# Conditional low-rank residual on one core: the second outer product of the first pair of blocks split into seven, and its sums divided between Pool and DVE

## The chip, the core and the metric

The kernel runs on one core of one Trainium2 chip. The metric is the device time of one execution in microseconds (us). The kernel before was timed three times; the comparison is with the median of those runs. A separate profiled execution gives the page and the trace that every duration below comes from.

## The reference

The input is 64 sequences of 64 tokens with 1024 features, 4096 tokens in all, in float32. Two layers follow each other, and each adds its result to its input:

```python
# layer 0: per sequence one adapter out of 64, rank 16
Bx = einsum('bni,bri->bnr', x, B[adapter_ids])
x = x + einsum('bnr,bor->bno', Bx, A[adapter_ids])
# layer 1: a dense product and eight gated experts of rank 16
base = einsum('btd,od->bto', x, W)
logits = einsum('btd,ed->bte', x, Wr) + 5.0 * one_hot(language_ids)
gates = softmax of the two largest logits, 0 elsewhere
h = einsum('btd,erd->bter', x, A1)
x = x + base + 2.0 * einsum('bter,bte,eor->bto', h, gates, B1)
```

The dense product with the 1024 x 1024 matrix W is most of the arithmetic.

## The kernel before

**Layout.** The kernel holds x with features on the partitions and tokens along the free axis. The 4096 tokens are eight blocks of 512, and two blocks make a pair; the variable s counts the four pairs, k the eight blocks. W lies in SBUF as sixteen tiles `w_ij` of 128 x 2 x 256. The identity is added to the four diagonal ones (`add_identity`), so that the dense product already contains the residual.

**Work per block.** `gather` (line 367) fetches the adapter's rows with an indirect DMA that Pool issues (`gb` for B, `ga` for A). `turn` transposes `gb` on TensorE (tiles `pt`), ScalarE (ACT) copies that to `bt`; `project` (line 400) multiplies it with x (tile `pb` out of `bt`, 64 small matmuls) and DVE masks the result to `bx`; `adapt` (line 428) multiplies `bx` with `ga` (tiles `px`) and DVE adds it to x in place. These steps are `early`. Then `rows` (line 466) multiplies x with the expert matrices and the gate matrix side by side (tiles `ph`), ACT copies the result to `h`, `gates` (line 504) is a chain of some twenty small DVE instructions that finds the two largest logits and scales `h`, and `weigh` (line 564) transposes `h` (tile `pg`) into `hg`. These are `late`.

**The dense product, twice by seven.** Of a pair, the product of a 2 x 2 arrangement of weights (halves of the outputs and of the features) with a 2 x 2 arrangement of tokens (halves of the features and the two blocks) is made with seven products and sums in place of eight. These are the outer products n, made in the order `ORDER` = 1, 2, 6, 7, 5, 3, 4. Their weights `m_q[n]` are sums of the quarters of W (`outer`, line 639); their tokens are x itself or sums of x: T3 = x_b[1] - x_b[0], T2 = T3 + x_a[0], T4 = x_a[1] - T2 and, in place, x_b[0] - x_a[0] (`token_sum`, line 696, four DVE instructions of 128 x 512 each; in the profile `t<-x,x`, `t<-t,x`, `t<-x,t`, `x<-x,x`). Each outer product is made in the same way again out of seven inner products k (`product`, line 833): each is eight matmul records of 128 x 256 in the trace, the two halves of the features for two groups of outputs, two records to each matmul instruction. The inner sums are

- of weights: `weights` (line 660), four instructions for each n, tiles `s_n5`, `s_n6`, `s_n7`, `s_n3` (profile: `s<-w,w`, `s<-s,w`, `s<-w,s`). They depend on W alone, so they are made in the first pair only, stored to DRAM (`s_kept`, DMAs that SP issues) and loaded again by the later pairs;
- of tokens: `inner_tokens` (line 718), four instructions for each n, tiles `ti_n5`, `ti_n6`, `ti_n7`, `ti_n4` (profile: `ti<-t`, `ti<-t,ti`, `ti<-x`, `ti<-x,ti`), made in every pair.

After a product, `leave` (line 866) adds what stands in PSUM to an output or to the sums `u` and `v`, on DVE, or on ACT where it is a plain copy. A PSUM tile `pa` gathers k = 1, 6, 5 and 3 and is read between these, so that each next one of them waits for the reading. Where an outer product takes part in one of the four results, four of its inner products carry two more matmuls with `b1_sb`, which add the experts (`hg`, or differences `hd`, `he` of it from `gate_sum` and `gate_diff`).

**Whole products.** An outer product that is named in `WHOLE` (line 250) is not split: `whole_product` (line 804) makes it in four parts with 128 x 512 matmuls (tiles `pw`), eight records each and two more with `b1_sb`. `WHOLE` has pair 0 with n = 1 and with n = 2. Their inner weight sums are made nevertheless, since the later pairs load them.

**What sets the order.** Nothing is issued by hand. Every step goes to a planner (class `Plan`, line 34) with the engines that may take it and its assumed cost there, the tiles that it reads and writes, the buffers that it takes and a due time `at`. `order` (line 64) goes through an assumed time and gives each engine the ready step that can start first, the earlier due time deciding between those that can start within 0.2; a step with two engines goes to the one where it can start first. The assumed cost of two SBUF-to-SBUF steps on DVE and Pool at once is raised. The result is one fixed order for each engine's queue. Buffers have fixed numbers (`slots`, line 256): two for each of `t5`, `t6`, `t7`, `t4` (the tiles `ti`), seven for `q` (halves of a block of x, and the sums T), two for PSUM `a`, two for `b`, two for `gb` and `ga`. A step that takes a buffer waits for the last reader of what was in it. `SLOTS` = 49 is the distance of two pairs in due times.

In the first pair the sums have the engines `BOTH` (DVE 0.7 or Pool 1.3); in the later pairs the inner token sums are Pool's. The driver at lines 988 to 1025 sets the due times; line 1009 is T4.

Of the kernel before, what the change touches and what calls it, by code (L numbers as in the profile page):

```python
# [177 lines left out]
def kernel(  # L178
# [68 lines left out]
    ORDER = (1, 2, 6, 7, 5, 3, 4)  # L247
    SLOTS = 49

    WHOLE = {(0, 1), (0, 2)}  # L250

    pe, dve = Pinned(tc, nc.tensor), Pinned(tc, nc.vector)
    act, pool, sp = Pinned(tc, nc.scalar), Pinned(tc, nc.gpsimd), Pinned(tc, nc.sync)
# [14 lines left out]
    def new(tag, shape, name):  # L268
        return pools[tag].tile(shape, F32, tag=tag, name=name)
# [74 lines left out]
    def part(t, cs=range(HC), gs=range(NG)):  # L344
        return [(t, c, g) for c in cs for g in gs]
# [7 lines left out]
    def load(k, i, at):  # L353
        t = ("x", k, i)

        def fn(e):
            made[t] = new("q", [P, HC, TB], f"x_{k}_{i}")
            sp.dma_start(
                made[t],
                xT[i * HC * P : (i + 1) * HC * P, k * TB : (k + 1) * TB].rearrange(  # L360
                    "(c p) t -> p c t", p=P
                ),
            )

        plan.add({"SP": 0.5}, fn, [], part(t), at, [("q", t)], kb=1024)

    def gather(k, tag, table, at):
        def fn(e):
            made[tag, k] = new(tag, [P, D], f"{tag}_{k}")
            pool.indirect_dma_start(  # L370
                out=made[tag, k],
                out_offset=None,
                in_=table,
                in_offset=bass.IndirectOffsetOnAxis(ap=idx[:, k : k + 1], axis=0),
            )

        plan.add({"POOL": 1.1}, fn, [], [((tag, k),)], at, [(tag, (tag, k))], kb=512)
# [204 lines left out]
    def early(k, at):  # L582
        turn(k, 0, at)
        turn(k, 1, at)
        project(k, at + 2)
        adapt(k, 0, at + 3)
        adapt(k, 1, at + 4)

    def late(k, at):
        rows(k, at)  # L590
        gates(k, at)
        weigh(k, at + 6)
# [32 lines left out]
    def combine(out, a, b, op, at, engines):  # L625

        fresh = out not in (a, b)

        def fn(e):
            if fresh:  # L630
                made[out] = new("s", [P, QC, QO], "_".join(str(p) for p in out))
            engine[e].tensor_tensor(made[out], made[a], made[b], op)

        plan.add(engines, fn, [(a,), (b,)], [(out,)], at, [("s", out)] * fresh, sb=True)

    DVE = {"DVE": 0.7}
    BOTH = {"DVE": 0.7, "POOL": 1.3}

    def outer(n, at):

        if n == 5:
            m_q[5] = {k: ("m5",) + k for k in quarter[1, 0]}
            for k in m_q[5]:
                combine(m_q[5][k], quarter[1, 0][k], quarter[1, 1][k], ALU.add, at, DVE)
        elif n == 7:
            m_q[7] = quarter[1, 0]
            for k in m_q[7]:
                combine(m_q[7][k], quarter[0, 0][k], m_q[7][k], ALU.subtract, at, DVE)
        elif n == 6:
            m_q[6] = quarter[0, 0]  # L650
            for k in m_q[6]:
                combine(m_q[6][k], m_q[5][k], m_q[6][k], ALU.subtract, at, DVE)
        elif n == 3:
            m_q[3] = quarter[0, 1]
            for k in m_q[3]:
                combine(m_q[3][k], m_q[3][k], m_q[6][k], ALU.subtract, at, DVE)
# [3 lines left out]
    def weights(s, n, at):  # L660

        out = {}
        if s > 0:
            for i, m in enumerate(ORDER):
                out[m] = t = ("s", s, n, m)

                def fn(e, t=t, m=m):
                    made[t] = new("s", [P, QC, QO], f"s_{s}_{n}{m}")
                    sp.dma_start(made[t].rearrange("p c o -> p (c o)"), s_kept[n - 1, m - 1])

                plan.add({"SP": 0.1}, fn, [("kept", n, m)], [(t,)], at + i - 8, [("s", t)], kb=256)
            wt[n] = out
            return
        m = m_q[n]
        out = {1: m[0, 0], 2: m[0, 1], 4: m[1, 1]}
        for k, (u, v, op) in {
            5: ((1, 0), (1, 1), ALU.add),
            6: (5, (0, 0), ALU.subtract),
            7: ((0, 0), (1, 0), ALU.subtract),
            3: ((0, 1), 6, ALU.subtract),  # L680
        }.items():
            out[k] = ("s", s, n, k)
            uu = m[u] if isinstance(u, tuple) else out[u]
            vv = m[v] if isinstance(v, tuple) else out[v]
            combine(out[k], uu, vv, op, at - 4, BOTH)
        for k in ORDER:
            t = out[k]

            def keep(e, t=t, k=k):
                sp.dma_start(s_kept[n - 1, k - 1], made[t].rearrange("p c o -> p (c o)"))  # L690

            plan.add({"SP": 0.1}, keep, [(t,)], [("kept", n, k)], at + 4, kb=256)
        wt[n] = out


    def token_sum(s, n, at):

        xa, xb = [("x", 2 * s, i) for i in range(2)], [("x", 2 * s + 1, i) for i in range(2)]
        u, v, op = {
            3: (xb[1], xb[0], ALU.subtract),  # L700
            2: (("t", s, 3), xa[0], ALU.add),
            4: (xa[1], ("t", s, 2), ALU.subtract),
            1: (xb[0], xa[0], ALU.subtract),
        }[n]
        t = xb[0] if n == 1 else ("t", s, n)
        for c in range(HC):

            def fn(e, c=c):
                if c == 0 and n != 1:
                    made[t] = new("q", [P, HC, TB], f"t_{s}_{n}")  # L710
                dve.tensor_tensor(made[t][:, c], made[u][:, c], made[v][:, c], op)

            plan.add(
                DVE, fn, part(u, [c]) + part(v, [c]) + (part(t, [0]) if c else []), part(t, [c]),
                at, [("q", t)] * (c == 0 and n != 1), sb=True,
            )

    def inner_tokens(s, n, m, at):
        def b(i, j):
            return made[m][:, i * QC : (i + 1) * QC, j * HT : (j + 1) * HT]  # L720

        def keys(i, j):
            return part(m, range(i * QC, (i + 1) * QC), range(2 * j, 2 * j + 2))

        out = {k: (("view", i, j), keys(i, j)) for k, i, j in ((1, 0, 0), (2, 1, 0), (3, 1, 1))}
        for k, u, v in ((5, (0, 1), (0, 0)), (6, (1, 1), 5), (7, (1, 1), (0, 1)), (4, (1, 0), 6)):
            t = ("ti", s, n, k)

            def fn(e, t=t, k=k, u=u, v=v):
                made[t] = new(f"t{k}", [P, QC, HT], f"ti_{s}_{n}{k}")  # L730
                vv = b(*v) if isinstance(v, tuple) else made["ti", s, n, v]
                engine[e].tensor_tensor(made[t], b(*u), vv, ALU.subtract)

            vk = keys(*v) if isinstance(v, tuple) else [(("ti", s, n, v),)]
            plan.add(
                {"POOL": 1.3} if s else BOTH, fn, keys(*u) + vk, [(t,)], at - 5,
                [(f"t{k}", t)], sb=True,
            )
            out[k] = (t, [(t,)])
        ti[n] = {  # L740
            k: ((lambda t=t: b(*t[1:])) if t[0] == "view" else (lambda t=t: made[t]), ks)
            for k, (t, ks) in out.items()
        }
# [33 lines left out]
    def products(s):  # L777
# [10 lines left out]
        def at():  # L788
            return s * SLOTS + slot[0]
# [131 lines left out]
        def begin(n):  # L921
            dest.setdefault(n, n)
            if s == 0 and n in (6, 3):
                outer(n, at() - 4)
            weights(s, n, at() + (6 if (s, n) in WHOLE else 0))
            if s == 0 and n == 2:
                outer(5, at() + 4)
                outer(7, at() + 8)
            if (s, n) in WHOLE:
                whole_h[n] = {2: ("hg", ka), 3: ("hg", kb), 7: ("hg", kb), 4: ("he", s)}.get(n)  # L930
# [31 lines left out]
        for n in ORDER:  # L962
            after = ORDER[ORDER.index(n) + 1] if n != ORDER[-1] else None
            if (s, n) in WHOLE:
                for k in rest:
# [35 lines left out]
    for s in range(NSUP):  # L1001
        k0 = 2 * s
        a0_ = s * SLOTS
        if s == 0:
            late(0, -14)
        late(k0 + 1, a0_ + 4 * (s > 0))
        token_sum(s, 3, a0_ + 3)
        token_sum(s, 2, a0_ + 5)
        token_sum(s, 4, a0_ + (18 if s == 0 else 7))
        token_sum(s, 1, a0_ + 20)  # L1010
        products(s)
        if s + 1 < NSUP:
            k0, k1 = k0 + 2, k0 + 3
            gather(k0, "gb", b0, a0_ + 8)
            gather(k0, "ga", a0, a0_ + 9)
            load(k0, 0, a0_ + 9)
            load(k0, 1, a0_ + 14)
            early(k0, a0_ + 17)
            late(k0, a0_ + 23)
            gather(k1, "gb", b0, a0_ + 22)  # L1020
            gather(k1, "ga", a0, a0_ + 23)
            load(k1, 0, a0_ + 22)
            load(k1, 1, a0_ + 29)
            early(k1, a0_ + 32)
# [48 lines left out]
```

## Time and profile before

| | |
|---|---|
| time, three runs | 528.14, 528.67, 529.69 us; median 528.67 |
| profiled execution, its own time | 528.18 us |
| its span | 526.4 us (1.78 us lie around it) |
| TensorE clock granted | 0.998 |
| PE (matmuls) busy | 507.3 us, 96% of the span |
| PEld (weight loads) busy | 433.9 us, 82% |
| DVE busy | 290.1 us, 55%, 554 instructions |
| Pool busy | 182.8 us, 35%, 149 instructions |
| ACT busy | 41.1 us, 8% |
| DMA | 99.19 MB, 188 GB/s in the mean |

How to read it: times are counted from the start of the span. A group is named by line, engine, operation and tiles, out before in; all compute instructions have line 29, the recording helper, so a group is known by its tiles. Since matmuls are pipelined, the duration of a matmul group reaches beyond the start of the next; what a product costs is read from start to start. In the view of waits a row says which engine waited for what, the sum in us, how often, and the longest.

### The profile page before, as it was taken

To read this page: it belongs to the slowest core of one execution; us is meant where nothing else is said; L and a number is where in the kernel's file an instruction comes from. 1 tells how busy PE (TensorE), PEld (TensorE's weight loads), DVE (VectorE), ACT (ScalarE), POOL (GpSimd) and SP (SyncE) were. 2 spreads that over 40 slices of the span, in tenths; PEclk is the share of its full clock that TensorE was granted. 3 is DMA by queue.
4 is the path that set the end of the run, shared out by engine and by line. 5 is a ranking of instruction groups with operands and counts; after the bars stand their busy time and mean duration, and the time that the engine had idled before them with its cause. 6 is when DMAs were issued, how large, how long until landed. Compare 5 with 4: busy or idle time off the path is not lost.

```text
span 526.4 us, 8463 instructions
## 1 busy us (share of the span) xinstructions
PE 507.3 (96%) x3400; PEld 433.9 (82%) x3400; DVE 290.1 (55%) x554; ACT 41.1 (8%) x81; POOL 182.8 (35%) x149
## 2 busy tenths in 40 slices
PE   2899999999999999999999999999999999999995
PEld 1755768798888988898888998889888898888884
DVE  0639999948964174616674355345567417432632
ACT  1111010002000100011000100000200010001000
POOL 3231955762343234222333313312422323433200
PEclk9999999999999999999999999999999999999999
DMA  8999735768666249735566526743546633610222
GB/s 291 362 364 401 273 135 189 271 226 305 217 202 210 82 113 321 262 106 184 177 190 207 184 82 212 268 159 122 164 161 197 207 92 103 216 42 1 80 81 80
DMA packets 53687, 99.19 MB, mean 188 GB/s; under 512 B 4880, under 2 KB 10000, under 8 KB 53648
## 3 DMA queue, kind: packets, MB, share of 16 engines
q1 hardware_dynamic: 51344, 90.26, 51.6%
q0 software_dynamic: 2304, 8.39, 4.4%
q8 instruction: 27, 0.44, 0.4%
q14 instruction: 12, 0.10, 0.0%
HBM read 69.01 MB, written 29.62 MB: 187 GB/s over the span
## 4 chain that ended last, share of the span: by engine, by line
PE 95%; DMA 2%; DVE 1%; issue 1%; SPq 0%; ACT 0%
PE pa L29 37%; PE pb L29 36%; PE ph L29 11%; PE pw L29 6%; PE px L29 3%; DMA ids_sb<-in_ids 2%; PE pt L29 1%; PE pg L29 1%; SPq L29 0%; DVE o L29 0%; DVE bias L29 0%; ACT o L29 0%; DVE lang L29 0%; DVE bx L29 0%
## 5 line engine op out<-in xcount | busy, mean ns | idle before, releaser
L29 PE MATMUL pa<-ti,s 128*128 128x256 f32 x416 | 99.0, 381 | 0.7 <-ACT o L29 0.7
L29 PE MATMUL pb<-ti,s 128*128 128x256 f32 x376 | 93.4, 380 | 0.0
L29 PEld LDWEIGHTS pa<-ti,s 128*128 128x128 f32 x416 | 77.6, 190 | 12.1 <-ACT o L29 1.1
L29 PEld LDWEIGHTS pb<-ti,s 128*128 128x128 f32 x376 | 70.7, 190 | 9.5
L29 POOL TENSOR_TENSOR ti<-x,ti 128x512 f32<-128x512 f32 x28 | 37.1, 1326 | 85.3 <-PE pb L29 84.3
L29 PEld LDWEIGHTS ph<-a_sb,x 128*128 128x128 f32 x512 | 62.7, 190 | 3.8 <-issue 2.7
L29 PE MATMUL ph<-a_sb,x 128*128 128x136 f32 x512 | 63.3, 279 | 2.1 <-issue 2.1
L29 POOL TENSOR_TENSOR ti<-t,ti 128x512 f32<-128x512 f32 x24 | 33.5, 1396 | 87.3 <-PE pb L29 64.9
L29 POOL TENSOR_TENSOR ti<-x 128x512 f32<-128x512 f32 x26 | 34.1, 1310 | 53.0 <-PE pb L29 31.6
L29 DVE TENSOR_TENSOR o<-pb,o 128x512 f32<-128x512 f32 x45 | 31.0, 690 | 34.1 <-PE pb L29 20.6
L29 PE MATMUL pa<-x,s 128*128 128x256 f32 x208 | 49.8, 379 | 0.0
L29 DVE TENSOR_TENSOR x<-px,x 128x512 f32<-128x512 f32 x64 | 39.8, 682 | 10.4 <-PE px L29 6.1
L29 POOL TENSOR_TENSOR ti<-t 128x512 f32<-128x512 f32 x22 | 29.4, 1339 | 44.1 <-PE pb L29 34.5
L29 PEld LDWEIGHTS pa<-x,s 128*128 128x128 f32 x208 | 38.7, 190 | 4.8
L29 PE MATMUL pa<-t,s 128*128 128x256 f32 x168 | 41.3, 382 | 0.8 <-DVE o L29 0.8
L29 PEld LDWEIGHTS pa<-t,s 128*128 128x128 f32 x168 | 31.4, 190 | 5.7 <-DVE o L29 1.2
L29 DVE TENSOR_TENSOR o<-pa,u 128x512 f32<-128x512 f32 x28 | 19.3, 691 | 26.8 <-PE pa L29 26.3
L29 PE MATMUL pw<-x,w 128*128 128x512 f32 x64 | 28.7, 595 | 0.0
L29 DVE TENSOR_TENSOR u<-pb,u 128x512 f32<-128x512 f32 x21 | 14.5, 689 | 25.5 <-ACT u L29 20.7
L29 PE MATMUL pb<-hg,b_sb 128*128 128x256 f32 x88 | 26.2, 379 | 0.0
L29 DVE TENSOR_TENSOR o<-pa,v 128x512 f32<-128x512 f32 x16 | 11.0, 690 | 27.3 <-PE pa L29 24.7
L29 PE MATMUL pb<-x,s 128*128 128x256 f32 x96 | 23.9, 381 | 0.0
(112 smaller groups left out, 578.9 us busy)
## 6 DMA issues: line engine op xcount, KB each, us to landing
s<-s_kept SPq DMA_DIRECT2D x147, 256.0 KB, 2.7
x<-in_xT SPq DMA_DIRECT2D x16, 1024.0 KB, 5.8
out_T<-o SPq DMA_DIRECT2D x32, 512.0 KB, 3.3
s_kept<-s SPq DMA_DIRECT2D x28, 256.0 KB, 3.8
s_kept<-w SPq DMA_DIRECT2D x18, 256.0 KB, 5.0
w<-in_w SPq DMA_DIRECT2D x16, 256.0 KB, 9.8
s_kept<-m SPq DMA_DIRECT2D x3, 256.0 KB, 5.1
a_sb<-in_a SPq DMA_DIRECT2D x1, 512.0 KB, 14.0
```

The lines of the kernel that those rows point to most:

```text
L29: return self._tc.keep_in_program_order(f(*args, **kwargs))
```

## The change

Four edits, all of which concern the first pair of blocks:

1. (0, 2) leaves `WHOLE`: the second outer product of the first pair is split into seven inner products like the later ones. `begin` then makes its inner token sums, four instructions, and one more gate difference (`hd`).
2. The inner sums of weights may go to Pool alone.
3. The inner sums of tokens of the first pair go to DVE alone.
4. The due time of T4 of the first pair is 25 in place of 18.

The due time of the weight sums of n = 2 also moves, since `begin` adds 6 to it for whole products.

```diff
-    WHOLE = {(0, 1), (0, 2)}
+    WHOLE = {(0, 1)}
...
     DVE = {"DVE": 0.7}
-    BOTH = {"DVE": 0.7, "POOL": 1.3}
+    POOL = {"POOL": 1.3}
...
-            combine(out[k], uu, vv, op, at - 4, BOTH)
+            combine(out[k], uu, vv, op, at - 4, POOL)
...
             plan.add(
-                {"POOL": 1.3} if s else BOTH, fn, keys(*u) + vk, [(t,)], at - 5,
+                POOL if s else DVE, fn, keys(*u) + vk, [(t,)], at - 5,
                 [(f"t{k}", t)], sb=True,
             )
...
-        token_sum(s, 4, a0_ + (18 if s == 0 else 7))
+        token_sum(s, 4, a0_ + (25 if s == 0 else 7))
```

Because the planner decides with these costs, the order of each queue changes between the first product of n = 2 and the first products of the second pair. In the new order:

- TensorE makes all four parts of n = 1, then n = 2 in seven products among the steps of block 1; from the first product of the second pair on its order is the one of before.
- Pool makes the weight sums of n = 1 and then of n = 2; behind them stand the gathers `ga` of block 3 and `gb` of block 4, and behind those the twelve sums of n = 6, 7 and 5. The eight sums of n = 3 and 4 follow.
- DVE makes the token sums of n = 2 where it made the weight sums of n = 1, T3 and T2 and the four token sums of n = 6 ahead of the gates of block 1, and T4 behind the token sums of n = 5.
- SP issues the four loads of the next pair's x behind the last store of the weight sums of n = 5, as before. The load that takes over the buffer of x_a[1], which T4 reads, is now the second of them; before, it was the first.

## The prediction

> **What bounds the kernel now.** I read the page's chain that ended last first, then TensorE's waits, then the timelines of the engines between 40 and 160 us, where the change lies.
>
> ```profile
> PE 95%; DMA 2%; DVE 1%; issue 1%; SPq 0%; ACT 0%
> ```
>
> The chain is TensorE nearly throughout. The view of waits of PE over the whole span says how little it ever waits:
>
> ```profile
> PE pt L29 <- DMA gb<-in_b,idx: 10.4, 1, 10.4
> PE ph L29 <- issue: 2.1, 1, 2.1
> PE pa L29 <- DVE o L29: 0.8, 1, 0.8
> PE pa L29 <- ACT o L29: 0.7, 1, 0.7
> PE px L29 <- DVE bx L29: 0.2, 1, 0.2
> ```
>
> The first two and the last end before 21 us and the 0.8 lies at 516 us, all outside the change; only the 0.7 (at 105.5 us) is in its reach. So PE work that is removed shortens the kernel, if DVE, Pool and the loads still deliver in time. The timeline of PE has the two kinds of product side by side (start, us, engine, group):
>
> ```profile
> 63.47 3.60 PE L29 MATMUL pw<-x,w 128*128 128x512 f32 x8
> 66.90 1.02 PE L29 MATMUL pw<-hg,b_sb 128*128 128x512 f32 x2
> 67.76 3.60 PE L29 MATMUL pw<-x,w 128*128 128x512 f32 x8
> ...
> 72.76 1.89 PE L29 MATMUL pa<-t,w 128*128 128x256 f32 x8
> 74.49 1.89 PE L29 MATMUL pb<-t,w 128*128 128x256 f32 x8
> 76.22 1.04 PE L29 MATMUL pt<-ident,gb 128*128 128x128 f32 x8
> ```
>
> From start to start a whole part costs 4.29 with its expert matmuls (63.47 to 67.76), an inner product 1.73 (72.76 to 74.49). The table by stretches (us, busy PE, PEld, DVE, ACT, POOL, clock, DMA) shows what reserve the helpers have there:
>
> ```profile
> 44.96:72.30 27.34, 27.25 (x170) 16.84 (x169) 25.83 (x42) 1.56 (x4) 17.19 (x12) 1.00 0.71 269
> 72.30:111.26 38.96, 38.28 (x288) 32.65 (x289) 34.61 (x47) 3.42 (x6) 27.81 (x20) 1.00 0.57 204
> 111.26:158.35 47.09, 47.09 (x362) 41.68 (x361) 33.59 (x62) 3.22 (x7) 15.90 (x13) 1.00 0.75 251
> ```
>
> DVE is full in the first two stretches. The timelines of DVE and Pool say why (DVE's line first):
>
> ```profile
> 54.26 5.99 DVE L29 TENSOR_TENSOR t<-x,x 128x512 f32<-128x512 f32 x4
> ```
> ```profile
> 53.42 1.27 POOL L29 TENSOR_TENSOR s<-w,w 128x512 f32<-128x512 f32 x1
> 54.65 1.71 POOL L29 TENSOR_TENSOR s<-w,s 128x512 f32<-128x512 f32 x1
> 56.32 1.71 POOL L29 TENSOR_TENSOR s<-w,w 128x512 f32<-128x512 f32 x1
> ```
>
> Beside Pool, four SBUF sums on DVE take 5.99; alone one takes 0.60 from start to start. Pool's grow from 1.27 to 1.71. Both together move on one instruction each per 1.67.
>
> [...] the sums above stretch, while DVE's additions out of PSUM keep 0.68 beside Pool. [...] here they alternate, and I price that with the measured 1.67. [...] a gather of Pool that waits for `pt` at 24 us holds the queue 5.4 us.
>
> **The split.** Four whole parts go: from their starts 4.49 (46.06), 4.39 (51.66), 4.29 (63.47) and 4.54 (67.76), 17.71 in all. Seven inner products come: 1.73 each, four of them 2.59 with the expert matmuls (the one at 141.08 starts 2.59 after that of 138.49), 3 x 1.73 + 4 x 2.59 = 15.55; where an inner product follows another kind of matmul it takes some 0.1 more (125.85 to 127.68 is 1.83), four times here: 15.95. PE saves 1.76, all on the path.
>
> **The ACT wait.** At 105.54 product k = 5 of n = 5 follows k = 6 in the same PSUM tile and waits 0.68 for ACT's copy. In the new order four other steps stand between. It falls to nothing: 0.68 saved; at worst it stays.
>
> **Pool.** It loses sixteen token sums and gains six weight sums. Those of n = 1 start behind a gather that ends at 26.3 and take 4 x 1.24, to 31.4; the weights that n = 2 needs land at 33.3, so its four sums run 33.4 to 38.4 as before. Meanwhile the gates of block 0 on DVE (29.3 to 33.0) may be held up to 2.1 by Pool; `pg` needs them at 44.4 and another load holds DVE until 37.8 anyway: no cost. Then comes the wait that is new: `gb` of block 4 waits until `pt` of block 2 has read the buffer, 69.6, and behind it in the queue stand twelve sums that Pool began at 50.84 before. The first follows at 70.6; with the 1.67 beside DVE the second, which PE needs for n = 6, k = 6 at 75.3, is ready at 73.7: 1.6 to spare. The twelfth ends at 70.6 + 15.0 (twelve at 1.25) + 3.3 (eight DVE sums let in at 0.41) = 88.9. The eight sums of n = 3 and 4 wait for DVE's update of `w` at 104.5 and end near 115; PE wants the first of them at 130.
>
> **DVE.** 24 token sums less six weight sums less the four token sums that it had, three more readings of PSUM and one `hd`: 18 more, some 11 us at 0.60. Walk the queue against PE. To 56.0 PE runs n = 1, k = 1, 2, 6, 7 of n = 2, and `px` exactly as long as before, `ph` again starts at 56.05. DVE has x of block 1 by 56.1; Pool is idle then, so T3, T2 and four token sums take 12 x 0.60, to 63.3, just as `ph` ends at 63.5. The gates follow the copy at 64.1 undisturbed: 3.87 (29.27 to 33.14 for block 0) and 0.6, to 68.6; `pg` wants them at 69.6: 1.0 to spare. Before, they lasted until 72.07, since one of them stood 3.15 beside Pool. One weight update and one PSUM reading later, at 69.9, PE wants the PSUM tile for k = 3 at 70.05: 0.15 to spare. From 70.6 to 88.9 eight DVE sums meet Pool's twelve. The release of PSUM for n = 7, k = 2 is due at 80.5 and comes at 78.2. The narrowest is the one for n = 5, k = 2: after PE's release at 84.9, DVE has two sums beside Pool (3.35), five without (3.0) and four PSUM readings (2.6), 8.95; PE arrives after 9.5: 0.5 to spare. The later ones have 1.0 or more. Three margins of 0.15, 0.5 and 1.0 in a walk that is good to half a microsecond: I allow 0.4 of new waits, from 0 to 1.5.
>
> **T4 later.** Its four sums move from 79.6 to 85.8 behind this knot, to 94 to 97; PE needs T4 near 138: no cost. But the load of the second half of block 2 waits for T4: issued at 97.2 instead of 90.29, landing after 5.7 at 102.9; `project` wants it at 105.8: 2.9 to spare. The first half waits in SP's queue for the last store of Pool's sums, 89, and lands by 95. SP's other stores only move.
>
> **Sum.** -1.76 - 0.68 + 0.4 = -2.04. From the second pair's first product (158.35, then 155.9) PE's order is the old one and it had one wait of 0.8. The span goes from 526.4 to 524.4, the profiled time from 528.18 to 526.1; the median lies 0.49 above the profiled execution, so 526.6.
>
> **Rivals.** *Eaten up:* the walk is half right, the readings for k = 3 and for n = 5 come 0.7 late each. For it: DVE has no slack at both places, and a DVE sum at Pool's start once took 2.19. Against: before, DVE was as full at 54 to 73 and PE never waited. -2.44 + 1.4 = -1.0, plus a gate wait of 0.3: 528.0. *Slower[...]:* if Pool's twelve sums end 5 us later, the five DVE sums I put behind them cost 1.67 too, 5 x 1.07 = 5.3, less 0.5 of reserve: PE stands 4.8 at n = 5, k = 2, and the time is 526.6 - 0.4 + 4.8 = 531.0. It decides as soon as Pool still adds at 90 us. For it: the twelve sums hang on one gather. Against: that gather waits only for `pt`, which nothing delays by 5 us. *No real saving:* weight loads (190 each) are nearly as long as a 128 x 256 record (216), so the split product could run at their pace. Against: the later n = 2 products already take 2.59 and 1.73. Then only 0.68 goes: 528.0.
>
> **Chances.** Forecast 0.60 (525.8 to 527.1), eaten up 0.22, slower 0.10, no saving 0.08. About 0.3%, 1.6 us, can be told from no change: below 527.1 is faster, 0.60; the second and fourth cases are the same, 0.30; slower 0.10. The range 525.6 to 529.0 takes in the forecast with its bounds (-2.44 with no wait is 526.2, less half a microsecond of reading error) and the two cases without change, and leaves out the slower one and the edges.
>
> **What would show it.** Right: PE's start of the second pair's first product near 155.9 with no wait over 0.5 before it; the ACT wait gone; gates of block 1 done before 69; Pool's twelve sums between 70.6 and 89. Wrong: a wait of `pa` or `pb` on DVE between 70 and 100, or of `pb` on a load of x near 106, or inner products of n = 2 with more than 2.6.

## The result, and the profile after

| | before | after |
|---|---|---|
| median (8 runs each) | 529.72 us (528.14 to 530.92) | 525.69 us (525.36 to 527.25) |
| ratio | | 0.9940, 95% interval 0.9928 to 0.9953 |
| profiled execution, own time | 528.18 | 525.91 |
| its span | 526.4 | 524.1 |
| first outer product to the second pair's first product | 28.66 to 158.35: 129.69 | 29.19 to 156.13: 126.94 |
| Pool busy | 182.8 | 167.7 |
| DVE busy | 290.1 | 294.0 |

By the ratio the change makes the kernel 0.6% faster, and the interval leaves out 1. One thing is needed to read the times: some executions of either kernel take about 1.6 us longer at a lower granted clock (in the mean 0.994 or 0.995 for two of the eight of the changed kernel, 0.997 to 0.999 for the others), and the two profiled executions above are not among them. The kernel before met this more often, to judge by its times, so the medians lie 4.0 apart, the ratio says 3.2, and the profiled spans say 2.3. The last experiments settle which is the change's own part, and what the clock does.

The chain that ended last, as the page has it, is TensorE as before; the 1% of "issue" is 0 now:

```profile
PE 95%; DMA 2%; DVE 1%; issue 0%; SPq 0%
```

The view of waits of PE over the whole span (engine, tile, releaser: us, times, longest):

```profile
PE pt L29 <- DMA gb<-in_b,idx: 10.6, 1, 10.6
PE ph L29 <- issue: 2.0, 1, 2.0
PE px L29 <- DVE bx L29: 1.6, 1, 1.6
PE pa L29 <- DVE o L29: 0.8, 1, 0.8
```

The wait for ACT is gone, and nothing has come in its place; the 0.8 lies at 513 us, as it did at 516 before. The wait of `px` for `bx`, at 17 us, has grown from 0.2 to 1.6. It lies ahead of everything that the change touches: `bx` stands in DVE's queue behind the steps that make the gates' bias, and these wait for their load.

The timeline of PE shows an inner product of n = 2 with its expert matmuls, and the place where the margin was 0.15 (start, us, engine, group):

```profile
53.94 1.13 PE L29 MATMUL pb<-ti,s 128*128 128x256 f32 x4
54.91 0.59 PE L29 MATMUL pb<-hg,b_sb 128*128 128x256 f32 x2
55.34 1.03 PE L29 MATMUL pb<-ti,s 128*128 128x256 f32 x4
56.20 0.59 PE L29 MATMUL pb<-hg,b_sb 128*128 128x256 f32 x2
...
70.10 0.60 PE L29 MATMUL pg<-ident,h 128*128 128x128 f32 x4
70.62 1.10 PE L29 MATMUL pa<-x,s 128*128 128x256 f32 x4
```

From 53.94 to the next group's start at 56.63 are 2.69. The seven take 1.82, 2.70, 1.82, 2.69, 1.72, 2.66 and 2.60, 16.01 together, where the whole product took 17.71. DVE's timeline is ahead of PE at each point:

```profile
56.66 2.50 DVE L29 TENSOR_TENSOR t<-x,x 128x512 f32<-128x512 f32 x4
...
68.58 0.69 DVE L29 TENSOR_TENSOR h<-h,s 128x512 f32<-128x512 f32 x1
...
69.79 0.68 DVE L29 TENSOR_TENSOR o<-pa,u 128x512 f32<-128x512 f32 x1
```

The four sums of T3 take 2.50 and not 5.99, for Pool is idle beside them (no instruction of it between 55.35 and 70.53). The gates' `h` is ready at 69.27, 0.83 before `pg`; the reading of PSUM ends at 70.47, 0.15 before the product that waits for it. Pool's timeline has what moved behind the gather:

```profile
70.53 0.94 POOL L29 DMA_INDIRECT gb<-in_b,idx  x1 [15.19 <-PE pt L29]
71.49 1.28 POOL L29 TENSOR_TENSOR s<-w,w 128x512 f32<-128x512 f32 x1
...
87.81 1.59 POOL L29 TENSOR_TENSOR s<-m,s 128x512 f32<-128x512 f32 x1
105.47 1.61 POOL L29 TENSOR_TENSOR s<-w,w 128x512 f32<-128x512 f32 x1 [16.06 <-PE pb L29]
```

The gather waits for `pt` (the value in brackets is the idle time before it and who ended it), the twelve sums run from 71.49 to 89.41. The table by stretches (us, busy PE, PEld, DVE, ACT, POOL, clock, DMA):

```profile
44.90:70.10 25.20, 25.20 (x209) 22.70 (x205) 23.08 (x54) 1.80 (x5) 0.96 (x1) 1.00 0.51 192
70.10:105.32 35.22, 35.22 (x166) 30.68 (x164) 30.41 (x43) 2.50 (x5) 18.54 (x13) 1.00 0.67 237
105.32:156.13 50.81, 50.81 (x485) 44.56 (x485) 40.96 (x77) 3.81 (x8) 20.86 (x16) 1.00 0.81 277
```

PE is busy to the last hundredth in all three; DVE has 2.1 and 4.8 us of reserve in the first two. Taking the time from each group's start to the next one's, by kind, over the stretch from the first outer product to the second pair's first product, the account of the two kernels is:

| us of TensorE | before | after |
|---|---|---|
| whole parts, matmuls with w | 27.86 | 13.83 |
| whole parts, expert matmuls | 3.78 | 0 |
| inner products | 59.08 | 70.55 |
| inner products, expert matmuls | 8.73 | 12.27 |
| `ph`, `px`, `project`, `pt` | 28.85 | 28.85 |
| `pg` | 1.39 | 1.45 |
| sum | 129.69 | 126.95 |

I call this stretch "the stretch" below. It leaves out the start, where the loads decide, and the rest, where nothing was changed (368.05 before, 367.97 after).

### The profile page after: what moved, and what is told of

Its sections match the earlier page's. It is cut to its first block, busy times and chain, and to the rows that moved or that the text cites. A ratio compares the mean times of both kernels' runs of the same rounds, so it can differ in the third digit from the quotient of the medians.

```text
span 524.1 us, 8532 instructions
## 1 busy us (share of the span) xinstructions
PE 504.3 (96%) x3432; PEld 439.6 (84%) x3432; DVE 294.0 (56%) x572; ACT 41.1 (8%) x81; POOL 167.7 (32%) x139
## 4 chain that ended last, share of the span: by engine, by line
PE 95%; DMA 2%; DVE 1%; issue 0%; SPq 0%
PE pa L29 39%; PE pb L29 37%; PE ph L29 11%; PE px L29 3%; PE pw L29 3%; DMA ids_sb<-in_ids 2%; PE pt L29 1%; PE pg L29 1%; SPq L29 0%; DVE o L29 0%; DVE bias L29 0%; DVE lang L29 0%; DVE bx L29 0%
## 5 line engine op out<-in xcount | busy, mean ns | idle before, releaser
L29 PE MATMUL pa<-ti,s 128*128 128x256 f32 x432 | 102.5, 381 | 0.0
L29 PE MATMUL pb<-ti,s 128*128 128x256 f32 x384 | 95.7, 380 | 0.0
L29 PEld LDWEIGHTS pa<-ti,s 128*128 128x128 f32 x432 | 80.7, 190 | 11.2 <-issue 0.2
L29 POOL TENSOR_TENSOR ti<-x,ti 128x512 f32<-128x512 f32 x24 | 30.9, 1288 | 78.8 <-PE pb L29 77.9
L29 POOL TENSOR_TENSOR ti<-t,ti 128x512 f32<-128x512 f32 x18 | 25.2, 1400 | 71.9 <-PE pb L29 54.8
L29 POOL TENSOR_TENSOR ti<-x 128x512 f32<-128x512 f32 x24 | 30.5, 1270 | 52.0 <-PE pb L29 35.9
L29 POOL TENSOR_TENSOR ti<-t 128x512 f32<-128x512 f32 x18 | 24.4, 1353 | 43.4 <-PE pb L29 33.9
L29 DVE TENSOR_TENSOR o<-pa,u 128x512 f32<-128x512 f32 x32 | 22.1, 690 | 26.1 <-PE pa L29 24.8
L29 PE MATMUL pb<-hg,b_sb 128*128 128x256 f32 x96 | 28.5, 379 | 0.0
L29 DVE TENSOR_TENSOR v<-pa,u 128x512 f32<-128x512 f32 x16 | 11.0, 689 | 24.4 <-PE pa L29 24.4
```

The source lines that it names most:

```text
L29: return self._tc.keep_in_program_order(f(*args, **kwargs))
```

## Experiments

My theory before the runs: the saving is TensorE work of the split and one wait; where the sums are made and when T4 is made saves nothing, but keeps the split from causing waits. The first four kernels take the change apart.

### The split alone

```diff
-    WHOLE = {(0, 1), (0, 2)}
+    WHOLE = {(0, 1)}
```

> The kernel before with the split of the second outer product alone; inner sums still on whichever of DVE and Pool the planner finds free, T4 early. My theory: the split saves 1.7 us of TensorE work and the ACT wait of 0.7 goes, but DVE and Pool now hand sums to each other (three of the four token sums of n = 6 on Pool, the weight sums of n = 6 on DVE behind the gates), so TensorE gets new waits on DVE or Pool of 1 to 3 us between 60 and 100 us: 526.5 to 528.5, slower than the changed kernel by 0.8 to 2.8. Rival (the split alone is the gain, the rest is decoration): 525.7 within 0.5, and no wait over 0.4 between 24 and 500 us. Rival (the gain comes from where the sums are made): 529 or more, no gain at all.

Measured: median 532.29 (lowest 530.72, highest 532.62), 1.0053 of before (95% interval 1.0034 to 1.0073); the stretch takes 131.03, 4.1 more than in the changed kernel. It is slower than doing nothing. The mechanism is the theory's, the size is above its range: 3.4 of new waits between 60 and 80 us (0.71, 2.32 and 0.38) where 1 to 3 were expected. By its number the second rival fits, that the gain comes from where the sums are made; the next experiment tests that. The timeline of PE has the largest wait:

```profile
75.17 1.99 PE L29 MATMUL pa<-ti,s 128*128 128x256 f32 x8 [2.32 <-DVE s L29]
```

and DVE's timeline what it waits for:

```profile
72.75 0.69 DVE L29 TENSOR_TENSOR s<-w,w 128x512 f32<-128x512 f32 x1
73.48 1.63 DVE L29 TENSOR_TENSOR s<-s,w 128x512 f32<-128x512 f32 x1
```

The weight sum that n = 6, k = 6 needs is made on DVE, behind the gates and beside Pool (1.63 instead of 0.60), and is done at 75.11. In the changed kernel Pool makes it, and PE never waits for it.

### The sums alone

```diff
-    BOTH = {"DVE": 0.7, "POOL": 1.3}
+    POOL = {"POOL": 1.3}
...
-            combine(out[k], uu, vv, op, at - 4, BOTH)
+            combine(out[k], uu, vv, op, at - 4, POOL)
...
-                {"POOL": 1.3} if s else BOTH, fn, keys(*u) + vk, [(t,)], at - 5,
+                POOL if s else DVE, fn, keys(*u) + vk, [(t,)], at - 5,
```

> The kernel before with the reassignment of the inner sums alone (weights on Pool, tokens on DVE); no split, T4 early. My theory: TensorE has the same work as before, so nothing can be saved but its 0.7 of waiting; Pool starts its nine weight sums near 51 us as before, DVE makes T3, T2 and four token sums more beside them, so the gates of block 1 end near 73 and pg waits about 1 us at 72 and DVE's readings of PSUM are late after it: 530 to 533, slower than before by 0.5 to 3. Rival (the gain is that the two engines no longer get into each other's way): faster than before by 1.5 or more, 526 to 528.

Measured: 528.94 (526.91 to 529.50), 0.9987 (0.9973 to 1.0000), and the stretch 128.41, 1.3 shorter than before. My theory fell here: I had it 0.5 to 3 slower. I left out that the planner knows DVE's load and moves TensorE's order with it: `pg` of block 1 stands behind two products of n = 6 now, at 78.29, and DVE's gates, done at 75.76, are in time. The rival (1.5 or more faster, since the engines keep out of each other's way) came closer, but 1.3 is less than it asked, and half of the change's 2.75 is still missing. By kinds, 1.10 of the 1.3 is in the inner products: the wait for ACT is gone, and TensorE changes between inner products and other kinds less often, each change costing about 0.1 (1.83 from 125.85 to 127.68 in the kernel before, against 1.73). So the wait that the change removes is removed by the assignment of the sums, through the order that the planner makes of it.

### Without the later T4

```diff
-        token_sum(s, 4, a0_ + (25 if s == 0 else 7))
+        token_sum(s, 4, a0_ + (18 if s == 0 else 7))
```

(against the changed kernel.)

> The changed kernel with T4 back at its early place; split and reassignment stay. My theory: the four sums of T4 stand again ahead of the sums that n = 5 and n = 7 need, and beside Pool's twelve sums they cost up to 1.67 each, 2.4 to 6.7 in all, against a reserve of 0.5 on DVE at n = 5, k = 2: new TensorE waits of 2 to 5 us between 78 and 105 us, 527.5 to 530.5. Rival (T4's place is of no consequence): 525.7 within 0.5, no new wait over 0.4.

Measured: 528.98 (527.63 to 530.04), 0.9993 (0.9979 to 1.0007); stretch 129.58, 2.6 longer than the changed kernel. The time is in my range and the mechanism is not mine. The timeline of PE:

```profile
97.19 1.97 PE L29 MATMUL pa<-ti,s 128*128 128x256 f32 x8 [0.72 <-issue]
99.09 1.08 PE L29 MATMUL pb<-x,bt 128*32 128x128 f32 x32
101.52 1.08 PE L29 MATMUL pb<-x,bt 128*32 128x128 f32 x32 [1.35 <-DMA x<-in_xT]
```

T4's sums on DVE are no wait. With T4 early the planner puts `project` of block 2 at 99 and not at 105, and it stands 1.35 waiting for the second half of x, a load issued behind the stores of Pool's sums. And the product at 97.19 follows k = 1 of n = 5 in the same PSUM tile directly, so that it waits for ACT's copy, which ends at 97.09 (the view calls it issue); in the changed kernel another product stands between the two, and there is no wait. A wait for ACT of the kind that the kernel before had is back.

### The first outer product split too

```diff
-    WHOLE = {(0, 1)}
+    WHOLE = set()
```

> The changed kernel with the first outer product split as well, so that all seven are. My theory (the saving is TensorE work, one whole product against seven inner ones): four whole parts without expert matmuls, 13.8 us together from 29.19 to 43.02, give way to seven inner products of 1.73 and some changes of kind, 12.3: 1.5 less, if the sums that PE needs are there; Pool has the second of the first four weight sums at 30.0 and PE wants it near 32.7, but DVE reads the first pb out of PSUM only behind the gates, after 41. So waits of 0 to 1.5: 524.2 to 525.7. Rival (the gain of the change came from the place of the second product only): 525.7 or more, with TensorE waiting 1.5 us or more on DVE or Pool before 45 us.

Measured: 532.34 (531.65 to 534.18), 1.0073 (1.0049 to 1.0097); stretch 132.00. The rival's number came (525.7 or more), but neither foresaw where it fails. Between 30 and 50 us PE waits no more than 0.3 at a time; it fails one block later, in the timeline of PE:

```profile
68.71 1.04 PE L29 MATMUL pg<-ident,h 128*128 128x128 f32 x4 [3.09 <-DVE h L29]
69.82 3.15 PE L29 MATMUL pa<-ti,s 128*128 128x256 f32 x8
```

From the end of `ph`, 62.4, DVE needs until 68.56 for the gates of block 1 with one sum among them, and the new order leaves only one inner product and `pt` to cover that, 3.2 us. And the eight records at 69.82 take 3.15 where they take 1.89 elsewhere, at a granted clock of 0.50 from 70 to 72: the second cost of a wait, taken up below.

### Split and later T4 without the reassignment

```diff
-    WHOLE = {(0, 1), (0, 2)}
+    WHOLE = {(0, 1)}
...
-        token_sum(s, 4, a0_ + (18 if s == 0 else 7))
+        token_sum(s, 4, a0_ + (25 if s == 0 else 7))
```

> The kernel before with the split and the later T4, the inner sums still on whichever of DVE and Pool the planner finds free. The split alone took 131.0 over the stretch, 4.1 more than the changed kernel, nearly all of it waits of pa on sums that DVE and Pool hand to each other between 68 and 78 us, well ahead of T4. My theory: T4's place can't mend that, so 130 to 132 and a wait of 2 or more before 80 us. Rival (the split needs only T4 out of the way): 128 or less.

Measured: 531.75 (530.66 to 532.51), 1.0060 (1.0046 to 1.0075); stretch 132.10, with the same wait of `pa` for a weight sum on DVE:

```profile
73.75 2.63 PE L29 MATMUL pa<-ti,s 128*128 128x256 f32 x8 [2.32 <-DVE s L29]
```

As the theory had it. The stretch is 1.07 longer than that of the split alone, and this is not T4's doing: behind the wait the granted clock is 0.50 for 3.4 us here and 1.00 there, and the same fourteen records behind it take 4.86 (73.75 to 78.61) in place of 3.74 (75.17 to 78.91, a wait of 0.38 among them).

### Reassignment and later T4 without the split

The two edits of the second and third experiment on the kernel before, T4 at 25.

> The reassigned sums and the later T4 without the split. The reassignment alone took the stretch from 129.7 to 128.4, since the wait for ACT was gone and there were four changes of kind of 0.1 less. My theory: T4 has nothing to add without the split, whose order of n = 5 and 7 is what it makes room for: 128.0 to 128.8, no wait over 0.4, and the whole change (126.9) is this plus the split's 1.7. Rival (T4's place saves time of its own): 127.5 or less.

Measured: 527.57 (526.91 to 529.02), 0.9982 (0.9969 to 0.9995); stretch 128.41, to the hundredth that of the sums alone. T4's place is worth nothing without the split. The three parts on the stretch, then (T4 later with neither of the others was not run):

| split | sums | T4 later | stretch |
|---|---|---|---|
| | | | 129.69 |
| yes | | | 131.03 |
| | yes | | 128.41 |
| | yes | yes | 128.41 |
| yes | | yes | 132.10, of it 1.1 half clock |
| yes | yes | | 129.58 |
| yes | yes | yes | 126.94 |

The split gives its 1.5 (128.41 to 126.94) only where both others stand.

### Pool longer, with and without reading

These two test the slower rival of the prediction: Pool's sums last beyond 90 us. The last weight sum of n = 5 is made five times over, with the same inputs and the same result:

```diff
+            for _ in range(4 if (n, k) == (5, 3) else 0):
+
+                def again(e, o=out[k], uu=uu, vv=vv, op=op):
+                    pool.tensor_tensor(made[o], made[uu], made[vv], op)
+
+                plan.add({"POOL": 0.0}, again, [(uu,), (vv,)], [(out[k],)], at - 4)
```

> The changed kernel with the last of Pool's twelve weight sums made five times over (same inputs, same result, nothing else late but its own store): Pool adds out of SBUF until some 95 us and not 89.4. From the first outer product's start to the second pair's first product the changed kernel takes 126.9. [...] the five DVE sums between 90.5 and 93.7 take up to 1.67 each and not 0.60, so DVE's reading of PSUM for n = 5, k = 2 comes 4 to 5 late against 0.55 of reserve: TensorE waits 3.5 to 4.7 near 95 us, the stretch takes 130.4 to 131.6. If a longer Pool queue by itself does no harm: no wait over 0.4, 126.9.

In the control, the same place has ten fills of a scratch tile:

```diff
+                def again(e):
+                    pool.memset(scratch, 0.0)
```

> The control of the longer sums: the same delay on Pool, but by ten fills of a scratch tile (128x512, nothing reads it) behind the last of the twelve weight sums. They read nothing from SBUF. If it is the reading that holds DVE up, DVE's sums between 90.5 and 93.7 stay at 0.60 from start to start, TensorE has no wait over 0.4 between 85 and 100 us and the stretch stays at 126.9 within 0.3. If any SBUF access of Pool holds DVE up, or Pool's lateness itself counts, TensorE waits as with the longer sums, 3 or more.

Measured: with the sums 530.59 (528.65 to 532.32), 1.0042 (1.0027 to 1.0058), stretch 131.84; with the fills 526.35 (525.53 to 527.30), 0.9955 (0.9940 to 0.9971), stretch 126.94, the changed kernel's to the hundredth. DVE's timeline with the longer sums:

```profile
93.01 1.64 DVE L29 TENSOR_TENSOR ti<-x,ti 128x512 f32<-128x512 f32 x1
94.57 1.75 DVE L29 TENSOR_TENSOR ti<-x 128x512 f32<-128x512 f32 x1
96.24 0.68 DVE L29 TENSOR_TENSOR ti<-x,ti 128x512 f32<-128x512 f32 x1
96.84 0.68 DVE L29 TENSOR_TENSOR u<-pb,u 128x512 f32<-128x512 f32 x1
```

and with the fills, which occupy Pool from 90.59 to 96.35:

```profile
93.03 0.69 DVE L29 TENSOR_TENSOR ti<-x,ti 128x512 f32<-128x512 f32 x1
93.64 0.69 DVE L29 TENSOR_TENSOR ti<-x 128x512 f32<-128x512 f32 x1
```

Beside sums of Pool a DVE sum takes 1.64 to 1.75, beside fills 0.69; by what way the sums slow each other was not shown. So the rival was right on the price of a DVE sum (it had 1.67) and on the place: the reading `u<-pb` comes at 97.52 and PE waits there. PE's timeline, and below it the table of stretches, with the clock as third number from the end:

```profile
97.67 3.20 PE L29 MATMUL pb<-x,m 128*128 128x256 f32 x8 [2.97 <-DVE u L29]
```
```profile
92.00:94.00 2.00, 2.00 (x11) 1.77 (x10) 1.97 (x2) 0.00 (x0) 1.92 (x2) 1.00 0.00 0
...
98.00:100.00 2.00, 2.00 (x7) 1.62 (x6) 2.00 (x5) 0.00 (x0) 0.00 (x0) 0.56 0.94 328
...
102.00:104.00 2.00, 2.00 (x11) 1.75 (x10) 0.89 (x2) 0.00 (x0) 0.00 (x0) 1.00 0.87 233
```

The wait is 2.97, below the 3.5 to 4.7 expected, and still the stretch is 4.9 longer: after the wait TensorE's granted clock is 0.50 from 98.2 to 101.6 us, and that is most of the rest.

### The wait for `bx`

```diff
-        plan.add({"DVE": 1.0}, languages, [("ids1",)], [("bias",)], -45)
+        return languages
...
-    consts()
+    languages = consts()
...
     early(0, -40)
+    plan.add({"DVE": 1.0}, languages, [("ids1",), (("bx", 0),)], [("bias",)], -30)
```

> The changed kernel with the three steps that make the gates' bias put behind the masked product of block 0 in DVE's queue, where they stood ahead of it and waited for their load. It bears on the 1.6 (0.2 in the kernel before) that TensorE waits for bx at 17 us. My theory: that wait is luck of the first loads and no part of the change; without it the first outer product starts up to 1.4 earlier (29.19 in the profile of the changed kernel), the stretch from there is unchanged, 126.9, and the time is 524.3 to 525.6 where the clock holds. Rival: the product behind it waits for its weights or for x instead and nothing is gained: 525.6.

Measured: 527.13 (525.47 to 529.57), 0.9963 (0.9952 to 0.9974); stretch 126.94. The wait for `bx` is gone, and `ph` behind it waits 3.3 for x instead of 2.0. The rival was right: nothing is gained. DVE's timeline shows why x is no earlier:

```profile
18.90 0.49 DVE L29 TENSOR_TENSOR w<-w,ident 128x128 f32<-128x128 f32 x2 [1.97 <-DMA w<-in_w]
19.31 4.87 DVE L29 TENSOR_TENSOR x<-px,x 128x512 f32<-128x512 f32 x8
```

The sums that finish x of block 0 stand in DVE's queue behind `add_identity`, which waits for a load of W; they begin at 19.31 here and at 19.28 in the changed kernel. (To move `add_identity` was not tried.) The median is even 1.4 higher than the changed kernel's, since 15 of the 22 executions lie at 526.95 or above. In this kernel's profiled execution the clock fell behind that wait (0.50 as third number from the end):

```profile
22.00:24.00 2.00, 2.00 (x11) 2.00 (x10) 2.00 (x4) 0.00 (x0) 0.00 (x0) 0.50 1.05 399
```

### The gap before `ph` filled

Over 85 executions of the kernel before, measured beside all experiments but the last (one more, of 1388.2 us, is left out), 46 lie between 527.86 and 529.11 (median 528.2) and 39 between 529.26 and 530.73 (median 529.8). The mean granted clock separates the two groups without an exception: 0.998 to 1.000 in the lower, 0.995 or 0.996 in the upper. To see whether the falling clock makes these two groups, and whether standing idle makes the clock fall, nine products of the identity with itself go where TensorE waits for x of block 0:

```diff
+            if (k, h) == (0, 0):
+                last = made[px[3]][:, HC - 1, :]
+                for _ in range(9):
+                    pe.matmul(last, ident, ident, start=True, stop=True)
+                pe.matmul(
+                    last, made["ga", k][3 * CG :, (HC - 1) * P : HC * P], made["bx", k][3 * CG :, :],
+                    start=True, stop=True, tile_position=(3 * CG, 0),
+                )
```

> The changed kernel with nine products of the identity with itself (128x128) added on TensorE in the 2.0 us near 19 to 21 us in which it waits for x of block 0; their result is overwritten by the last adapter product, made once more. Every kernel so far has runs in two groups some 1.6 us apart, and in the profiles of the upper group TensorE's granted clock is 0.50 for about 3 us behind that wait, as it is behind waits of 3 us elsewhere (first outer product split too, longer sums). My theory: the clock falls because TensorE stood idle, and what the kernels' medians have beyond the change itself (3.2 where the stretch differs by 2.7) is that they fell into this a different number of times. With the gap filled all runs lie in the lower group, 525.3 to 526.1. Rival (the clock falls by itself, whatever TensorE does): two groups as before, 525.5 and 527.2, a median between.

> The kernel before with the same nine products in the same gap. By my theory all its runs lie in its lower group, 527.9 to 528.9, and the changed kernel with the gap filled is 2.7 faster than it, as the stretch from the first outer product to the second pair's first product says (126.9 against 129.7). Rival: two groups, 528.2 and 529.8. If the change gains more than its stretch shows, the two filled kernels differ by 3.2 or more.

Measured: the changed kernel filled 526.05 (525.82 to 526.38), 0.9950 (0.9935 to 0.9964); the kernel before filled 528.59 (528.24 to 529.03), 0.9996 (0.9987 to 1.0004). None of the 20 executions lies in an upper group; of the kernel before, on the same chip and interleaved with them, 10 of 27 do. The table of stretches of the changed kernel, filled:

```profile
22.00:24.00 2.00, 2.00 (x20) 2.00 (x19) 2.00 (x5) 0.00 (x0) 0.94 (x1) 1.00 1.04 382
```

Twenty `ph` records fit into 2 us, against 11 at 0.50 (22 to 24 us in the kernel above). The two filled kernels differ by 2.54, and their stretches by 2.41 (129.35 and 126.94): that is what the change itself is worth. The theory said 2.7, from a profile of the kernel before whose stretch is 0.34 longer than the filled one's (129.69; most of it a short wait for the gates, below). The 3.2 of the ratio is too much.

Nine were more than the gap needed, so the last kernel has seven:

> The changed kernel with seven products in the gap instead of nine. With nine the first ph product began at 21.69, 4.62 after the first px product (17.07); without any it began 4.07 after (17.19, 21.26): the filling was 0.55 too long. Seven are 0.49 shorter. My theory: the clock still holds in all runs and the time falls by what was too long, from 526.05 to 525.5 or 525.6, the lower group of the changed kernel and under its median of 525.69. Rival: the gap needs to be filled to its end, so some runs lie at 527.2 again.

Measured: 525.57 (525.36 to 526.32), 0.9937 (0.9921 to 0.9952), six executions, none in the upper group. The median of the changed kernel itself, 525.69, is not clearly higher, but two of its eight executions were at 527.2 and none of these is. It is the best version found.

## Why the prediction was right

The median came at 525.69 where 526.6 was forecast, inside the range of 525.6 to 529.0 and close to its lower end. The mechanism was right: TensorE's work on the second outer product became less, a wait went, and none came in its place. By its steps:

- **The split, -1.76.** 17.71 went and 16.01 came, -1.70. But 0.25 of the 17.71 was no work. In the timeline of PE of the kernel before, the last expert matmuls take 1.11 to the next group's start, and those at 66.90 take 0.86:

```profile
71.19 1.02 PE L29 MATMUL pw<-hg,b_sb 128*128 128x512 f32 x2
72.30 0.63 PE L29 MATMUL pg<-ident,h 128*128 128x128 f32 x4
```

`pg` waited for the gates' `h`, done on DVE at 72.15; the wait is too short for the view of waits, and the prediction took it for work and named the 0.7 as the only wait in the change's reach. The split by itself is thus worth 1.45, which agrees with the 1.47 between the fourth and the last row of the table (128.41 to 126.94). The other 0.25 goes because the gates come in time. In the filled kernel before they did as well: the row of expert matmuls of whole products is 3.53 there and not 3.78. An inner product with expert matmuls takes 2.60 to 2.70. The prediction named more than 2.6 as a sign of being wrong; its own 2.59 with 0.1 for a change of kind is already more, so this sign tells nothing.
- **The ACT wait, -0.68.** Right in size; the record at which PE waited took 0.84 more than its like:

```profile
102.98 1.89 PE L29 MATMUL pa<-ti,s 128*128 128x256 f32 x8
105.54 1.99 PE L29 MATMUL pa<-ti,s 128*128 128x256 f32 x8 [0.68 <-ACT o L29]
```

That the new order removes it was right too, but the order comes from the assignment of the sums and is kept by the later T4, not by the split, as the second and third experiment show.
- **The allowance, +0.4.** This is the term of the sum that was mis-sized: it measured 0. The three margins held: 0.15 at k = 3 of n = 2 as forecast, 0.58 at n = 5, k = 2 (94.29 against PE at 94.87; forecast 0.5), 0.83 at the gates (forecast 1.0).
- **Sum.** On the stretch -2.75 was measured where -2.04 was forecast. It is -1.70 for n = 2, -1.00 for the inner products of the other n (0.84 of it at the record that waited, the rest fewer changes of kind), -0.09 for n = 1 and +0.05 for `pg`. The profiled times differ by only 2.27, since the changed kernel's first outer product began 0.53 later (29.19 against 28.66): the load of W for which DVE waits ahead of the sums of x let it go on at 18.87, against 18.34. So it is in part luck that the profiled execution came within 0.2 of its forecast (525.91 against 526.1): the stretch saved 0.7 more than forecast, and the start gave 0.5 of that back.
- **From profile to median, +0.49.** Wrong in kind: this difference is not a property that carries over from one kernel to the next. It depends on how often the clock fell. The changed kernel's median lies 0.22 below its profiled execution, and that is most of the 0.9 between the forecast and the measured median.
- **Pool.** Twelve sums from 71.49 to 89.41 (forecast 70.6 to 88.9), the first weights in time by 1.4 (forecast 1.6). One size was wrong and did no harm: beside Pool's sums of n = 1 and 2 the gates' step `w<-ex,w` of block 0 ended 7.85 after the gates' start, against 3.42 before, so they were held up 4.4 and not at most 2.1; DVE then still waited 0.53 for a load of W.
- **DVE.** It has 18 instructions more, as forecast, but its busy time rose by 3.9 and not by 11, since more of its sums stand where Pool is idle (T3: 2.50 for 5.99).
- **T4.** The load of the second half of block 2 issued at 97.49 and landed at 103.02 (forecast 97.2 and 102.9), `project` began at 105.32.
- **The rivals.** Nothing was eaten up. Pool's sums stayed harmless since they ended at 89.4; the longer sums show that they decide where the prediction put it, with a wait of 2.97 and 1.9 more, most of it the clock of 0.50, in place of 4.8 of wait. The split does save.

## What to carry to other kernels

Where a planner sets the order, an edit that only says which engine may take a step can move the order of the busiest engine; compare that order before pricing the edit, and do not call a part useless because it saves nothing alone. On an engine that is hardly ever idle, count the work from start to start by kind, and look for a group that takes longer than its like, which is a wait that the view may leave out: the account above gives 2.74 of the 2.75 on the stretch, where the medians said 4.0 and the ratio 3.2. Here a wait of TensorE of 2 us cost its length and, in 39 of 85 executions of the kernel before, some 1.6 us more at a lower granted clock; harmless products in the gap avoided that in all of 26 executions.

## What the runs showed of the hardware

**A granted clock of 0.50 lasted 3.4 us each time.** With Pool's longer sums the clock falls at 98.23 and is back at 101.65. The tables of stretches give the same for the other falls ahead of the last product, by the shares of 1.00 and 0.50 in them: 22.08 to 25.48 in the split alone, 21.00 to 24.40 and 68.80 to 72.20 with the first outer product split too. The two falls of that last trace begin 47.80 apart, which is 14 times 3.414; the kernel before and the changed kernel, without a fall, have the full clock for 508.59 us, 149 times 3.413, from 15.57 and from 13.72 on.

**It came behind idle time of TensorE.** The split alone and the split with the later T4 have the same wait of 2.32. The table of stretches, in steps of 3.41 us counted from the times at which the clock changes in each trace, shows the stretch with the wait and the next one (PE's busy time is the first number behind the comma, the clock the third from the end). The split alone:

```profile
73.27:76.68 3.41, 1.51 (x7) 1.36 (x8) 3.34 (x3) 0.00 (x0) 3.41 (x3) 1.00 0.88 341
76.68:80.09 3.41, 3.03 (x15) 2.38 (x14) 2.98 (x5) 0.00 (x0) 3.33 (x3) 1.00 0.42 163
```

The split with the later T4:

```profile
71.55:74.97 3.42, 1.22 (x6) 1.09 (x7) 3.35 (x3) 0.00 (x0) 3.42 (x3) 1.00 0.89 347
74.97:78.38 3.41, 3.41 (x9) 2.45 (x8) 3.27 (x5) 0.00 (x0) 3.33 (x3) 0.50 0.48 186
```

In the first the boundary of two steps divides the wait, 1.90 of idle time lie in the stretch, and the clock of the next is 1.00; in the second 2.20 lie in it, and the clock of the next is 0.50. Eight falls ahead of the last product stand in the tables that were taken, in the traces of seven experiments, and the 3.41 us ahead of each hold 2.0 to 3.3 of idle time. In the changed kernel a stretch with 1.35 of idle time and 2.07 of `px` products with 32 rows (17.14 to 20.55) was followed by no fall.

The wait of 2.05 near 20 us is divided too in the profile of the kernel before, at 18.99 (steps counted from 15.57; 1.74 of idle time in the later stretch), and the clock holds. An estimate from these numbers, for the two groups: if the boundary lies anywhere with equal chance, and the clock falls from an idle time on that lies between 1.90 and 2.00, a wait of 2.05 has that much in one stretch in 43 to 49 of 100 executions; 39 of 85 were measured. That idle time of this length always brings a fall was not shown.
